# Reordering the opening, the set-up products and the last pair's pieces of a convolution block

## The chip, the cores and the metric

The kernel runs on one NeuronCore of a Trainium2 chip. The core has five engines that run their own instruction streams and meet through semaphores: TensorE (PE, matrix products from SBUF into PSUM), VectorE (DVE), ScalarE (ACT), GpSimd (POOL) and SyncE (SP). The last three, and in this kernel ScalarE at two places, also issue DMA transfers. The metric is the time of one execution on the device in microseconds, the median of several runs. Everything is computed in float32.

## The reference

The input x has 16 images of 192 channels with 64 × 64 pixels. Two layers follow each other.

```python
# layer 0
h = ln2d(x)                                    # over channels
pg = conv1x1(h, in_proj_w, in_proj_b)          # 192 -> 384
projected, gate = split(pg, 2, axis=1)
projected = dwconv3(projected, dw_k)           # depthwise 3x3
scanned = directional_scan(projected, ...)     # four recurrences, left, right, down, up, mixed
local = dwconv3(projected, le_k)
mixed = (scanned + local) * sigmoid(gate)
mixed = gelu(batch_norm(mixed))                # statistics over all images and pixels
x = x + conv1x1(mixed, out_proj_w, out_proj_b)
h2 = ln2d(x)
x = x + conv1x1(gelu(conv1x1(h2, fc1_w, fc1_b)), fc2_w, fc2_b)   # 192 -> 768 -> 192
# layer 1
t = relu(bn(mean over pixels(x) @ w1.T))       # 48 values an image
wt = (t @ w2.T + b2)                           # a 3x3 kernel for each image and channel
out = depthwise conv of x with wt, masked to 4 of the 9 taps, + bias
```

The batch norm needs all images, so the work falls into a part before it and one after it. The kernels of layer 1 need the mean of a whole image, so an image pair's output can be made only when its last pixel of layer 0 is there.

## The kernel before, in words

The function is conv_block_kernel. Images are taken in eight pairs, and 64 channels of the one image lie in partitions 0 to 63, of the other in 64 to 127 (HALF); the index t counts three groups of 64 channels. The order of instructions on all engines is the one in which the program writes them (manual_schedule), so where a call stands in the text is where it stands in its engine's queue.

**First stage**, 64 chunks of 512 pixels of a pair. load_a (L463) brings a chunk in by six transfers, three on the sync queue and three on the GpSimd queue, into one of four xa buffers. turn (L476) transposes it on PE (L481). variance (L485, L488 and L489 on DVE) and deviation (L491: a square root on ACT, L493, and a reciprocal on DVE, L494) give the scale of the layer norm. project (L497) makes the products with the weights wi (L509 on PE), and DVE (L514) and ACT (L515) scale them out of PSUM into stg or mid, in turns of four chunks. store and store_first (L524, L530) write these to DRAM and to the tile low.

Ahead of the loop, projection_weights (L270) scales the weights by the norm's weight (L275, DVE), forms their mean over channels by products (L278, PE), and its result, called centre at L555, subtracts it (L279, DVE).

The other set-up work is spread over the chunks by a table: beside(n, f) puts f behind chunk n's own instructions. The entries that the change touches are these.

- decays (L281): sigmoid and tanh on ACT, six small DVE instructions, and an exponential on ACT, beside chunk 0. gains (L292), beside chunk 1, needs its results.
- sums_across(k) (L357): three transposes on PE (L360) into a PSUM tile from bank(), and a copy out by DVE (L361). conv_bias(k) (L363) is one product (L365, PE) and copies out (L317, DVE). They stand beside chunks 11 and 12, 13 and 14, 15 and 16.
- positions(k) (L394): three transposes on PE (L397) into a tile from bank(), and a copy by ACT (L399). It stands beside chunks 11, 13, 15, 17, 24, 26, 30 and 34. All of bank() is one PSUM bank.
- runs(t) (L382): DVE only, beside chunks 20 to 22.
- finish_weights (L131): with k = 0, beside chunk 50, the scale s1 of the squeeze on ACT and DVE and the share of the norm's bias in the hidden layer's bias by 18 products of one column (L139, PE) with an addition on DVE (L141); with k = 1 to 3, beside chunks 51 to 53, the scaling of wf1 by the norm's weight on DVE (L143).

**Second stage**, 96 steps k of two channels each, from k = −2. depthwise(k+2) (L602) makes products on PE (L612) from low, pg_o or mid into ps_d, and ACT adds the bias (L625, L627). tables(k+1) writes decay tables by ACT (L635), scans(k+1) runs two recurrences on DVE (L647, L649), local and vertical multiply on PE (L656, on quarters of the array: 64 rows by 64 columns), sigmoid is on ACT (L677), gate on DVE (L690, L691). The first depthwise needs what store_first wrote last into low (L527).

**Third stage**, 64 chunks again: out projection (L855, L859), norm (L882 to L910), the hidden layer first (L920, with ACT's L923) and second (L817), final (L941). At the end of a pair, pooled, squeeze and excite give the kernels (taps, L970).

**Last pair.** Its output is made after the loop by dynamic_last (L986), for four row groups g of 16 rows and three channel groups t, into a tile ol from a ring of four buffers (tag gl). With dg None, ACT makes the first tap with the bias (L995) and DVE adds three taps (L65, 128 × 1024 each). With dg, PE makes the piece by products with the taps on a 128 × 128 diagonal, eight products into two PSUM banks (ps_d, L1002), and ACT evicts them with the bias (L1003). Before, t = 2 is on PE and t = 0 and 1 are on DVE. Each piece leaves by two transfers (L1006), on the sync queue for DVE's pieces and on GpSimd for PE's.

```python
    dynamic_last(n_pairs - 1, 0, 0, None)
    for g in range(NG):
        dynamic_last(n_pairs - 1, g, 1, None)
        if g + 1 < NG:
            dynamic_last(n_pairs - 1, g + 1, 0, None)
        dynamic_last(n_pairs - 1, g, 2, dg)
```

Of the kernel before, what the change touches and what calls it, by code (L numbers as in the profile page):

```python
# [27 lines left out]
C = 192  # L28
HW = 64
# [26 lines left out]
def conv_block_kernel(ctx: ExitStack, tc: tile.TileContext, x, prm, w_in, w_out, w_fc1, b_fc1, w_fc2, w1, bn1, w2, out):  # L56
# [73 lines left out]

    def finish_weights(k, pb):  # L131

        if k == 0:
            nc.scalar.activation(s1, b1[:, 3:4], AF.Sqrt, bias=eps5[0:RED])
            nc.vector.reciprocal(s1, s1)
            nc.vector.tensor_mul(s1, s1, b1[:, 0:1])
            for m in range(NFC):
                for t in range(3):
                    nc.tensor.matmul(pb[:, m:m + 1], wf1[0:64, t, 128 * m:128 * m + 128],  # L139
                                     pt3[0:64, t, LN2B:LN2B + 1], start=(t == 0), stop=(t == 2))  # L140
            nc.vector.tensor_add(bf1, bf1, pb[:, 0:NFC])  # L141
        else:
            nc.vector.tensor_scalar_mul(wf1[:, k - 1], wf1[:, k - 1], pt3[:, k - 1, LN2W:LN2W + 1])  # L143

# [99 lines left out]
    with ExitStack() as stage:  # L244
# [22 lines left out]
        def bank():  # L267
            return psa.tile([128, CH], F32, tag="pb", name="pb")

        def projection_weights():  # L270

            by_group = lambda v: v.rearrange("p (k g c) -> p g k c", k=2, c=GC)
            flat = lambda v: v.rearrange("p g k c -> p (g k c)")
            for t in range(3):
                nc.vector.tensor_scalar_mul(wi[:, t], by_group(w0[:, t]), pt3[:, t, LN1W:LN1W + 1])  # L275
            pc = bank()
            for t in range(3):
                nc.tensor.matmul(pc[:, 0:2 * C], mean_w, flat(wi[lo, t]), start=(t == 0), stop=(t == 2))  # L278
            return lambda: [nc.vector.tensor_sub(flat(wi[:, t]), flat(wi[:, t]), pc[:, 0:2 * C]) for t in range(3)]  # L279

# [135 lines left out]
        def beside(n, f, *args):  # L416
            side.setdefault(n, []).append((f, args))

        beside(0, decays)
        beside(1, gains)  # L420
# [8 lines left out]
        for k in range(3):  # L429
            beside(11 + 2 * k, sums_across, k)  # L430
            beside(12 + 2 * k, conv_bias, k)
        for k, n in enumerate((9, 11, 13, 15, 19, 24, 28, 32)):
# [13 lines left out]
        beside(49, load_lm, 1)  # L446
        beside(50, lambda: finish_weights(0, bank()))
        for k in range(3):
            beside(51 + k, finish_weights, k + 1, None)

# [98 lines left out]
        for c in range(3):  # L549
            load_a(c)  # L550
        centre = projection_weights()
        turn(0)
        for g in range(AR):
            variance(0, g)
        centre()  # L555
        deviation(0)
# [24 lines left out]
    with ExitStack() as stage:  # L581
# [163 lines left out]
        for k in range(-2, n_bp + 1):  # L745
# [14 lines left out]
            if 0 <= k + 1 < n_bp:  # L760
                scans(k + 1)
            if k + 2 < n_bp:
                depthwise(k + 2)
            if 0 <= k < n_bp:
                local(k)
                sigmoid(k)
            if k == n_bp - 5 * hp_:
                spread(0)
# [216 lines left out]

    def dynamic_last(p, g, t, dg):  # L986

        xi, taps, r = ximg[p % n_img], pst[p]["taps"], g * GR
        o = wp.tile([128, GR, HW], F32, tag="gl", name="ol", bufs=4)
        src = lambda k, r0, nr: xi[:, t, r0 + k // 3:r0 + k // 3 + nr, k % 3:k % 3 + HW]  # L990
        if dg is None:
            for k in range(NTAP):
                w = taps[:, t, k:k + 1]
                if k == 0:
                    nc.scalar.activation(o, src(k, r, GR), AF.Identity, bias=pt3[:, t, BIAS:BIAS + 1], scale=w)  # L995
                else:
                    stt(o, src(k, r, GR), w, o)
        else:
            ps = ps2.tile([128, 2, CH], F32, tag="f1", name="ps_d", bufs=2)
            for h in range(2):  # L1000
                for k in range(NTAP):
                    nc.tensor.matmul(rows(ps[:, h]), dg[:, k], src(k, r + h * CR, CR), start=(k == 0), stop=(k == NTAP - 1))  # L1002
            nc.scalar.activation(o.rearrange("p h w -> p (h w)"), ps.rearrange("p k n -> p (k n)"), AF.Identity,  # L1003
                                 bias=pt3[:, t, BIAS:BIAS + 1])
        for i, q in enumerate(HALF):
            (nc.sync if dg is None else nc.gpsimd).dma_start(ov[2 * p + i, 64 * t:64 * t + 64, r * HW:(r + GR) * HW],  # L1006
                                                             o[q].rearrange("p h w -> p (h w)"))

# [51 lines left out]

    dg = mxs[0].rearrange("p t n -> p (t n)")[:, 0:NTAP * 128].rearrange("p (k m) -> p k m", k=NTAP)
    for k in range(NTAP):
        nc.vector.tensor_scalar_mul(dg[:, k], ident, pst[n_pairs - 1]["taps"][:, 2, k:k + 1])
    dynamic_last(n_pairs - 1, 0, 0, None)
    for g in range(NG):
        dynamic_last(n_pairs - 1, g, 1, None)
        if g + 1 < NG:
            dynamic_last(n_pairs - 1, g + 1, 0, None)
        dynamic_last(n_pairs - 1, g, 2, dg)

# [41 lines left out]
```

## Time and profile before

The three runs before took 3830.37, 3835.88 and 3836.39 us; the median is 3835.88 us. The profiled execution has a span of 3826.1 us.

| stretch of the span | us from its start | PE busy | DVE busy | ACT busy | DMA share |
|---|---|---|---|---|---|
| opening | 0 to 20 | 7.38 of 20 | 5.48 | 1.55 | 0.96 |
| first stage | 200 to 400 | 198.69 of 200 | 155.10 | 80.77 | 0.98 |
| second stage | 800 to 1000 | 200.00 of 200 | 198.04 | 170.40 | 1.06 |
| third stage | 2000 to 3000 | 1000.00 of 1000 | 635.86 | 392.32 | 0.24 |
| end | 3790 to 3826 | 22.46 of 36 | 24.37 | 10.11 | 0.63 |

The DMA share is the mean busy share of the core's 16 DMA engines; values over 1 come from its reckoning. In the lines of the timeline and of the groups, an entry has the engine, the line of the program, the operation, the tile written and the tiles read with their shapes, and the number of instructions; what stands behind it in brackets is the idle time of the engine just before and what ended it. Each float32 product shows as two records on PE. The chain follows the work that ended last back from release to release.

### The profile page before, as it was taken

The numbers are of one execution on the slowest core, as the hardware profiler recorded it, in microseconds if no ns is written. First come the engines' busy times: TensorE is split into PE (matmuls) and PEld (weight loads), VectorE is DVE, ScalarE is ACT, GpSimd is POOL, SyncE is SP. The second block draws the span as 40 slices with busy tenths as digits, with TensorE's granted clock in tenths as the row PEclk, the third lists the DMA queues.
The fourth block names the chain that finished last, engine by engine and source line by source line (L and its number), as shares of the span: only waits on it lengthen the run. The fifth ranks groups of instructions, "written<-read, shape, count | busy, mean of one in ns | idle before, by whom it ended". The sixth has DMA issues, their size and how long they took to land.

```text
span 3826.1 us, 61482 instructions
## 1 busy us (share of the span) xinstructions
PE 3764.0 (98%) x25484; PEld 1762.9 (46%) x25484; DVE 2676.8 (70%) x4140; ACT 1780.3 (47%) x1879; POOL 420.2 (11%) x683
## 2 busy tenths in 40 slices
PE   8999999999999899999999999999999999999998
PEld 5566666776555433333333333333333333333333
DVE  6787776999999964556656656756665766674764
ACT  3343434888888733333434434434343433343342
POOL 2334332010010110000000000000000000000000
PEclk9999999999999999999999999999999999999999
DMA  6899998999999741112212212222222221221212
GB/s 158 227 252 238 275 263 254 296 283 274 285 275 268 209 91 34 43 39 73 74 48 61 77 53 64 64 67 60 64 56 67 70 63 49 79 72 39 69 28 72
DMA packets 307526, 491.14 MB, mean 128 GB/s; under 512 B 46432, under 2 KB 202416, under 8 KB 307248
## 3 DMA queue, kind: packets, MB, share of 16 engines
q1 hardware_dynamic: 249424, 294.88, 28.7%
q0 software_dynamic: 57408, 191.99, 18.9%
q8 instruction: 202, 3.31, 0.4%
q14 instruction: 76, 0.62, 0.1%
q10 hardware_dynamic: 416, 0.33, 0.0%
HBM read 284.91 MB, written 197.92 MB: 126 GB/s over the span
## 4 chain that ended last, share of the span: by engine, by line
PE 95%; DMA 2%; DVE 2%; issue 0%; ACT 0%; POOL 0%; SPq 0%; POOLq 0%; DVEq 0%; ACTq 0%
PE ps_f L920 27%; PE ps_f L817 26%; PE ps_pj L509 12%; PE ps_l L656 10%; PE ps_d L612 6%; PE ps_o L859 5%; PE ps_o L855 3%; PE ps_xt L481 2%; PE ps_v L882 1%; PE ps_m L882 1%; DMA xa<-in_x_dram 0%; PE ps_k L817 0%; DVE ol L65 0%; DVE v L647 0%; DMA ximg<-mixed_d 0%
## 5 line engine op out<-in xcount | busy, mean ns | idle before, releaser
L920 PE MATMUL ps_f<-h,wf 64*128 64x512 f32 x4608 | 1050.1, 600 | 5.1 <-DVE h L910 4.6
L817 PE MATMUL ps_f<-gl,place 128*64 128x512 f32 x4608 | 1021.5, 592 | 0.0
L923 ACT ACTIVATE gl<-ps_f,bf 128x1024 f32<-128x1024 f32 x384 | 428.0, 1115 | 1163.1 <-PE ps_f L920 1162.4
L920 PEld LDWEIGHTS ps_f<-h,wf 64*128 64x128 f32 x4608 | 433.5, 187 | 564.5 <-issue 563.2
L862 DVE SCALAR_TENSOR_TENSOR ximg<-ps_o,pt,low 128x256 f32<-128x256 f32 x384 | 168.3, 481 | 626.5 <-PE ps_o L859 623.7
L817 PEld LDWEIGHTS ps_f<-gl,place 128*64 128x64 f32 x4608 | 330.5, 137 | 580.0 <-issue 537.9
L509 PE MATMUL ps_pj<-wi,xa 64*128 64x384 f32 x3072 | 515.9, 488 | 3.4 <-DVE stg L514 3.4
L509 PEld LDWEIGHTS ps_pj<-wi,xa 64*128 64x128 f32 x3072 | 294.3, 187 | 197.1 <-issue 12.3
L65 DVE SCALAR_TENSOR_TENSOR o<-ximg,taps,o 128x1024 f32<-128x1024 f32 x252 | 323.8, 1285 | 85.7 <-ACT o L980 78.2
L984 POOL DMA_DIRECT2D out_dram<-o x168 | 87.9, 528 | 2134.1 <-DVE o L65 2131.3
L909 DVE RECIPROCAL rs<-rs 128x512 f32<-128x512 f32 x64 | 214.3, 3349 | 64.4 <-ACT rs L908 64.4
L647 DVE TENSOR_TENSOR_SCAN v<-tab,q 128x1024 f32<-128x1024 f32 x96 | 218.3, 2274 | 10.7 <-ACT tab L635 10.7
L649 DVE TENSOR_TENSOR_SCAN v<-tab,q 128x1024 f32<-128x1024 f32 x96 | 217.5, 2265 | 0.0
L635 ACT ACTIVATE tab<-mask,dec_b 128x1024 f32<-128x1024 f32 x192 | 209.0, 1138 | 0.0
L859 PE MATMUL ps_o<-low,wo 128*64 128x256 f32 x1536 | 209.0, 393 | 0.0
L515 ACT ACTIVATE stg<-ps_pj,rsa 128x384 f32<-128x384 f32 x128 | 120.2, 943 | 189.6 <-PE ps_pj L509 176.6
L515 ACT ACTIVATE mid<-ps_pj,rsa 128x384 f32<-128x384 f32 x128 | 120.9, 944 | 182.5 <-PE ps_pj L509 172.2
L488 DVE BATCH_NORM_STATS2 st<-ps_xt 128x6 f32<-128x192 f32 x512 | 173.9, 340 | 24.0 <-PE ps_xt L481 24.0
L891 DVE TENSOR_TENSOR h<-ximg,ps_m 128x768 f32<-128x768 f32 x128 | 116.1, 948 | 98.7 <-PE ps_m L882 98.7
L237 DVE STREAM_TRANSPOSE low<-low 128x512 f32<-128x512 f32 x174 | 167.6, 1014 | 2.1 <-issue 0.3
L469 POOL DMA_DIRECT2D xa<-in_x_dram x192 | 119.8, 630 | 369.1 <-PE ps_pj L509 308.3
L941 DVE SCALAR_TENSOR_TENSOR ximg<-ps_f,pt,ximg 128x512 f32<-128x512 f32 x192 | 134.1, 748 | 36.2 <-PE ps_f L817 35.8
(198 smaller groups left out, 4143.4 us busy)
## 6 DMA issues: line engine op xcount, KB each, us to landing
low<-in_x_dram SPq DMA_DIRECT2D x128, 384.0 KB
out_dram<-o POOLq DMA_DIRECT2D x168, 256.0 KB, 3.7
mid<-pg_d SPq DMA_DIRECT2D x8, 4096.0 KB
low<-mixed_d SPq DMA_DIRECT2D x116, 256.0 KB
low<-pg_d SPq DMA_DIRECT2D x7, 4096.0 KB
pg_o<-pg_d SPq DMA_DIRECT2D x7, 4096.0 KB
xa<-in_x_dram POOLq DMA_DIRECT2D x192, 128.0 KB, 6.1
xa<-in_x_dram SPq DMA_DIRECT2D x192, 128.0 KB
```

Of the source, the lines that this page charges most:

```text
L65: nc.vector.scalar_tensor_tensor(o, in0, scalar, in1, ALU.mult, ALU.add, **kw)
L509: nc.tensor.matmul(ps[i], pixels(n, t, g)[q], wi[q, t].rearrange("p g k c -> p (g k c)"), start=(t == 0), stop=(t == 2))
L515: nc.scalar.activation(stag[blk][1][:, :, j], ps[1], AF.Copy, scale=rs[:, g, 1:2])
L612: nc.tensor.matmul(dst(ps[o, ih]), mats[g % 2]["dm"][q, di + 1, :, ch], src(s["pg"][q, :, 0, ch]), start=(di == 0), stop=stop)
L647: nc.vector.tensor_tensor_scan(vf, tab, q, 0.0, ALU.mult, ALU.add)
L649: nc.vector.tensor_tensor_scan(vf[:, ::-1], tab[:, ::-1], q[:, ::-1], 0.0, ALU.mult, ALU.add)
L656: nc.tensor.matmul(dst(bst[k]["ps"][i][o]), lm_of(g)[q, m, :, c], src(q, ih), start=start, stop=stop)
L817: nc.tensor.matmul(ps[q], w(i), rhs(i), start=start, stop=stop)
L859: nc.tensor.matmul(ps[q, wh].rearrange("p (r w) -> p r w", w=32), wo[:, 64 * t:64 * t + 64], cols(rows(s["mx"][:, i]))[:, :, wh], start=Fa ...
L909: nc.vector.reciprocal(rs, rs)
L920: nc.tensor.matmul(pf[:, i], wf1[q, t, 128 * m:128 * m + 128], s["h"][q, t], start=(t == 0), stop=(t == 2))
L923: nc.scalar.activation(gl, pf, AF.Gelu, bias=bf1[:, m:m + 1])
```

## The change

The opening is put in another order: projection_weights becomes a generator that runs in three steps, and decays() runs ahead of the loop instead of beside chunk 0. sums_across and conv_bias move from chunks 11 to 16 to chunks 18 to 23, of which none has a positions. finish_weights is split in three: squeeze_scale stays beside chunk 50, hidden_bias (PE and DVE) goes to the beginning of the second stage, ahead of its first depthwise, and scale_hidden, now on ACT, goes to steps 1, 3 and 5 of the second stage. In the last pair PE makes seven pieces and DVE five. PE's pieces are made by products on quarters of the array: 16 of 64 rows by 64 columns with the diagonal's halves, where the two halves of the rows of pixels go to the two halves of the PSUM partitions. Such a piece leaves by four transfers, over two queues; the last three use ScalarE's and sync's queues, the others GpSimd's and sync's. The purpose is to fill or shorten the times in which PE waits.

```diff
-    def finish_weights(k, pb):
-        if k == 0:
...
-        else:
-            nc.vector.tensor_scalar_mul(wf1[:, k - 1], wf1[:, k - 1], pt3[:, k - 1, LN2W:LN2W + 1])
+    def squeeze_scale():
+        nc.scalar.activation(s1, b1[:, 3:4], AF.Sqrt, bias=eps5[0:RED])
+        nc.vector.reciprocal(s1, s1)
+        nc.vector.tensor_mul(s1, s1, b1[:, 0:1])
+    def hidden_bias(pb):
+        for m in range(NFC):
+            for t in range(3):
+                nc.tensor.matmul(pb[:, m:m + 1], wf1[0:64, t, 128 * m:128 * m + 128],
+                                 pt3[0:64, t, LN2B:LN2B + 1], start=(t == 0), stop=(t == 2))
+        nc.vector.tensor_add(bf1, bf1, pb[:, 0:NFC])
+    def scale_hidden(t):
+        nc.scalar.activation(wf1[:, t], wf1[:, t], AF.Copy, scale=pt3[:, t, LN2W:LN2W + 1])
@@ projection_weights
             for t in range(3):
                 nc.vector.tensor_scalar_mul(wi[:, t], by_group(w0[:, t]), pt3[:, t, LN1W:LN1W + 1])
+            yield
             pc = bank()
             for t in range(3):
                 nc.tensor.matmul(pc[:, 0:2 * C], mean_w, flat(wi[lo, t]), start=(t == 0), stop=(t == 2))
-            return lambda: [nc.vector.tensor_sub(flat(wi[:, t]), flat(wi[:, t]), pc[:, 0:2 * C]) for t in range(3)]
+            yield
+            for t in range(3):
+                nc.vector.tensor_sub(flat(wi[:, t]), flat(wi[:, t]), pc[:, 0:2 * C])
+            yield
@@ the table
-        beside(0, decays)
         beside(1, gains)
...
-            beside(11 + 2 * k, sums_across, k)
-            beside(12 + 2 * k, conv_bias, k)
+            beside(18 + 2 * k, sums_across, k)
+            beside(19 + 2 * k, conv_bias, k)
...
-        beside(50, lambda: finish_weights(0, bank()))
-        for k in range(3):
-            beside(51 + k, finish_weights, k + 1, None)
+        beside(50, squeeze_scale)
@@ ahead of the chunks
-        centre = projection_weights()
+        steps = projection_weights()
+        next(steps)
+        decays()
         turn(0)
+        next(steps)
         for g in range(AR):
             variance(0, g)
-        centre()
+        next(steps)
         deviation(0)
@@ second stage
             if 0 <= k + 1 < n_bp:
                 scans(k + 1)
+            if k == -2:
+                hidden_bias(psb.tile([128, CH], F32, tag="l", name="pb_h", bufs=4))
             if k + 2 < n_bp:
                 depthwise(k + 2)
             if 0 <= k < n_bp:
                 local(k)
                 sigmoid(k)
+            if k in (1, 3, 5):
+                scale_hidden(k // 2)
@@ dynamic_last
             ps = ps2.tile([128, 2, CH], F32, tag="f1", name="ps_d", bufs=2)
-            for h in range(2):
-                for k in range(NTAP):
-                    nc.tensor.matmul(rows(ps[:, h]), dg[:, k], src(k, r + h * CR, CR), start=(k == 0), stop=(k == NTAP - 1))
+            for k in range(NTAP):
+                for i, q in enumerate(HALF):
+                    for h in range(2):
+                        nc.tensor.matmul(rows(ps[HALF[h], i]), dg[q, k, q], src(k, r + h * CR, CR)[q],
+                                         start=(k == 0), stop=(k == NTAP - 1))
...
-        for i, q in enumerate(HALF):
-            (nc.sync if dg is None else nc.gpsimd).dma_start(...)
+        for i in range(2):
+            if dg is None:
+                nc.sync.dma_start(ov[2 * p + i, 64 * t:64 * t + 64, r * HW:(r + GR) * HW], o[HALF[i]].rearrange("p h w -> p (h w)"))
+            for h in range(2 if dg is not None else 0):
+                r0 = r + h * CR
+                queues[h].dma_start(ov[2 * p + i, 64 * t:64 * t + 64, r0 * HW:(r0 + CR) * HW],
+                                                  o[HALF[h], i * CR:(i + 1) * CR].rearrange("p h w -> p (h w)"))
@@ after the loop (last = n_pairs - 1)
+    dg2 = taps_on_diagonals(0)
+    dynamic_last(last, 0, 0, None)
+    dg1 = taps_on_diagonals(1)
+    dynamic_last(last, 1, 0, None)
+    dynamic_last(last, 0, 2, dg2)
+    dynamic_last(last, 1, 2, dg2)
+    dynamic_last(last, 2, 0, None)
+    dynamic_last(last, 2, 2, dg2)
+    dynamic_last(last, 3, 0, None)
+    dynamic_last(last, 3, 2, dg2)
+    dynamic_last(last, 0, 1, None)
+    for g in range(1, NG):
+        dynamic_last(last, g, 1, dg1, (nc.scalar, nc.sync))
```

More of the change, by code (lines that the diff above doesn't have):

```diff
@@ L129, in load_weights @@
                 nc.sync.dma_start(pv[q, 1], prm[128:C])
-    def finish_weights(k, pb):
-        if k == 0:
[L134 to L141, printed above, removed]
-        else:
-            nc.vector.tensor_scalar_mul(wf1[:, k - 1], wf1[:, k - 1], pt3[:, k - 1, LN2W:LN2W + 1])
+    def squeeze_scale():
[10 more added lines that the diff above has]
+        nc.scalar.activation(wf1[:, t], wf1[:, t], AF.Copy, scale=pt3[:, t, LN2W:LN2W + 1])
     n_blk = n_half * NB
@@ L984, in dynamic, with dynamic_last @@
             nc.gpsimd.dma_start(ov[2 * p + i, 64 * t:64 * t + 64, r * HW:(r + GR) * HW], o[q].rearrange("p h w -> p (h w)"))
-    def dynamic_last(p, g, t, dg):
+    def dynamic_last(p, g, t, dg, queues=(nc.gpsimd, nc.sync)):
         xi, taps, r = ximg[p % n_img], pst[p]["taps"], g * GR
@@ L999, in dynamic_last @@
             ps = ps2.tile([128, 2, CH], F32, tag="f1", name="ps_d", bufs=2)
-            for h in range(2):
-                for k in range(NTAP):
-                    nc.tensor.matmul(rows(ps[:, h]), dg[:, k], src(k, r + h * CR, CR), start=(k == 0), stop=(k == NTAP - 1))
+            for k in range(NTAP):
[3 more added lines that the diff above has]
+                                         start=(k == 0), stop=(k == NTAP - 1))
             nc.scalar.activation(o.rearrange("p h w -> p (h w)"), ps.rearrange("p k n -> p (k n)"), AF.Identity,
                                  bias=pt3[:, t, BIAS:BIAS + 1])
-        for i, q in enumerate(HALF):
-            (nc.sync if dg is None else nc.gpsimd).dma_start(ov[2 * p + i, 64 * t:64 * t + 64, r * HW:(r + GR) * HW],
-                                                             o[q].rearrange("p h w -> p (h w)"))
+        for i in range(2):
[5 more added lines that the diff above has]
+                                                  o[HALF[h], i * CR:(i + 1) * CR].rearrange("p h w -> p (h w)"))
     def at(f, n, *a):
@@ L1059, in conv_block_kernel, with taps_on_diagonals @@
         at(bn_gelu, late_)
[L1061 to L1069, printed above, removed]
+    last = n_pairs - 1
+    def taps_on_diagonals(j):
+        dg = mxs[j].rearrange("p t n -> p (t n)")[:, 0:NTAP * 128].rearrange("p (k m) -> p k m", k=NTAP)
+        for k in range(NTAP):
+            nc.vector.tensor_scalar_mul(dg[:, k], ident, pst[last]["taps"][:, 2 - j, k:k + 1])
+        return dg
+    dg2 = taps_on_diagonals(0)
[11 more added lines that the diff above has]
+        dynamic_last(last, g, 1, dg1, (nc.scalar, nc.sync))
 def _layout(i):
```

## The prediction

> **What bounds the kernel.** I read the page's busy time and chain first, then the busy time of stretches of 20 us, then the timeline and the chain at the four places that the change touches.
>
> ```profile
> PE 3764.0 (98%) x25484; PEld 1762.9 (46%) x25484; DVE 2676.8 (70%) x4140; ACT 1780.3 (47%) x1879; POOL 420.2 (11%) x683
> PE 95%; DMA 2%; DVE 2%; issue 0%; ACT 0%; POOL 0%; SPq 0%; POOLq 0%; DVEq 0%; ACTq 0%
> ```
>
> TensorE (PE) is busy 98% of the span and 95% of the chain. So time is won only where PE idles, or runs work that needn't be on its path: at the opening, beside some chunks of the first stage, at the seam to the second stage, and after the last chunk. The first is seen in the timeline (start, duration, engine, line, then the idle time before it and who ended it):
>
> ```profile
> 8.86 4.21 PE L278 MATMUL pb<-wi,wf 64*128 64x384 f32 x6 [8.86 <-DVE wi L275]
> 12.99 2.82 PE L481 MATMUL ps_xt<-ident,xa 128*128 128x128 f32 x12
> 19.58 2.80 PE L481 MATMUL ps_xt<-ident,xa 128*128 128x128 f32 x12 [3.76 <-DVE st L488]
> 22.30 9.25 PE L509 MATMUL ps_pj<-wi,xa 64*128 64x384 f32 x48
> ```
>
> PE starts at 8.86, runs the mean products before the first transposes, then sits 3.76 us while VectorE (DVE) takes chunk 0's variances. The next view is the chain in chunks 10 to 13 (start, duration, what):
>
> ```profile
> 131.96 7.99 PE ps_pj L509 x48
> ...
> 140.68 0.33 ACT rsa L493
> 141.01 0.03 issue
> 141.03 0.20 DVE rsa L494
> 141.24 0.22 DVE wf L361
> ...
> 141.50 0.40 PE pb L397 x3
> 141.90 1.46 PE ps_xt L481 x12
> 143.36 7.94 PE ps_pj L509 x48
> 151.30 0.52 PE pb L365 x2
> ```
>
> A plain chunk is 7.94 + 1.46 = 9.40 us. Here L397 waits for a PSUM bank whose reader, the copy L361, stands behind the reciprocal, so PE leaves its own work for ACT and DVE. The chain around chunk 50 shows the bias products of finish_weights:
>
> ```profile
> 511.06 7.94 PE ps_pj L509 x48
> 518.99 3.91 PE pb L139 x35
> 522.90 2.45 PE ps_xt L481 x12
> 525.35 8.58 PE ps_pj L509 x48
> ```
>
> and the timeline the seam and the end:
>
> ```profile
> 649.52 9.17 PE L612 MATMUL ps_d<-low,dm 64*64 64x512 f32 x110 [2.20 <-DMA low<-mid]
> 3783.19 29.27 PE L1002 MATMUL ps_d<-ximg,low 128*128 128x512 f32 x64 [0.75 <-PE ps_k L817]
> 3784.03 30.80 DVE L65 SCALAR_TENSOR_TENSOR ol<-ximg,taps,ol 128x1024 f32<-128x1024 f32 x24 [0.46 <-ACT ol L995]
> 3798.09 1.24 ACT L995 ACTIVATE ol<-ximg,pt,taps 128x1024 f32<-128x1024 f32 x1 [3.89 <-DMA out_dram<-ol]
> 3813.52 1.11 ACT L1003 ACTIVATE ol<-ps_d,pt 128x1024 f32<-128x1024 f32 x1 [4.35 <-DMA out_dram<-ol]
> ```
>
> PE and DVE end there together (3812.5 and 3814.8), but ACT waits for output buffers too.
>
> **What the Trainium skill says.** "TensorEngine Tiling (Array Packing)", section Tiling Modes: in 64×64 mode there are four tiles that run in parallel. The trace agrees: L656 is of this kind, and its chain pieces are 36 records in 3.86 us, 0.107 us each, against 0.43 us between L1002's weight-load pairs, 0.215 each, at full width. "TensorE: Matmul & The Clock Gate", section Part 1: after an idle window of about 3.4 us the array runs at half rate until about as long a busy one. It agrees: chunk 0's and 1's transposes take 2.8 us against 1.46, and L1002's first pairs are 0.85 us apart. "DMA: Bandwidth & Descriptors", section on the anatomy of one DMA: about 2.0 us of a transfer's time is fixed, whatever its size. The trace has 4.4 to 5.1 us from a GpSimd issue of 256 KB to landing, which is consistent with it.
>
> **The change, part by part.**
>
> Opening. Order on PE becomes transposes of chunk 0, mean products, transposes of chunk 1. The sync queue's own issues show when chunk 0's three pieces land, as each of the issues at 9.40, 11.37 and 13.51 waited for one. So the first transposes go piece by piece and end at 13.5 + 0.9 = 14.4 instead of 15.8. Mean products: 14.4 to 18.6 at the half rate of before (4.2). The variances (3.7 us, 8 x 0.46) run beside them, 14.4 to 18.1. The centring needs the products, so its first third ends at 19.1, hidden by chunk 1's transposes: 18.6 to 21.4 cold, 20.1 warm. Chunk 0's projection then starts at 20.1 to 21.4 against 22.30, and a PE without the 3.76 us gap should be warm sooner, worth up to the 1.24 us by which L509's first chunk (9.18) exceeds 7.94. Bounds 0.9 and 3.4; I take 2.2. decays() moves ahead of the transposes: its six DVE instructions (1 us) and two table loads (1.28 us each) run before 13.5, while DVE and ACT have nothing to do; chunk 2's 0.57 us excess (9.97 against 9.40), which a table load in front of L493 caused, goes. Together −2.8, bounds −1.5 and −4.
>
> Sums across. With sums_across and positions in one chunk the period is 11.40 (131.96 to 143.36), 11.39 and 11.40: 2.00 over plain. A chunk with positions alone (195.91 to 205.49) is 9.58, 0.18 over. So chunks 11, 13, 15 win 3 x 1.82 = 5.5. The moved sums cost 0.2 to 0.3 each in chunks 18, 20, 22, where no second user waits for the bank: +0.8. The conv_bias products cost 0.52 a chunk before and after. DVE has room for runs() there: it is 70 to 80% busy in this stage. Net −4.7.
>
> Hidden bias. Chunk 50 took 14.29 us and chunk 51 10.04 instead of 9.40: −5.5 in all, because the one-column products leave the clock low. At the seam they wait for the same release as depthwise(0) did, the last eviction of the first stage at 646.13, and take 4.1 us: depthwise then starts at 650.3, instead of 649.52 with 0.8 us of it already done. Cost +1.6, as 2.5 of the 4.1 us lie in the wait for low<-mid. Net −3.9. What is queued behind them on PE is depthwise alone; the addition to bf1 on DVE has nobody waiting.
>
> Scaling of wf1. Three DVE multiplications leave chunks 51 to 53, where DVE has slack: 0. Three ACT instructions enter the second stage at k = 1, 3, 5. Nearest row: L923, 1024 elements in 1.115 us, so about 0.9 each. Behind each stand tables(k+2) on ACT, and scans(k+2) on DVE wait for them; ACT is 74% busy in 600 to 800 us, PE carries the chain. +0.3, bounds 0 and 2.7.
>
> End. PE's pieces go from 4 to 7, each 16 quarter products, 32 records of 0.107 = 3.4 us instead of 7.3, and 7 of them are 24 us with about 1.7 more cold. DVE's go from 8 to 5 of 3.85 us: 19.3 plus two sets of diagonals of 0.87. So both engines could be done by 3808. But a piece holds one of four buffers until its output has landed. From the timeline the DVE pieces land about 6.3 us after their last operation (3791.8 to 3798.09, 3799.4 to 3805.79), PE's 5 to 6 after theirs. Buffer time before: 8 x (1.2 + 3.9 + 6.3) + 4 x (1.1 + 6) = 119.6; after: 5 x 11.4 + 7 x (1.1 + 6.6) = 110.9, where 1 us is for the sync queue, on which half of each PE piece waits behind a DVE piece. Over four buffers: 29.9 against 27.7, −2.2; bounds 0 (1.3 us more on the landing of each of the seven PE pieces would undo it) and −6 (both engines free). I take −2.
>
> First stage's transfers. DMA share is 0.9 to 1.07 from 200 to 520 us, and PE there lost twice 1.7 us to late stores. What chunks 11 to 16 save comes off a stretch (140 to 200) with 12% DMA slack, 7 us; the moved work gives 2 us of room back at 205 to 255. Chunk 50's stall let the queues catch up (share 0.63 at 520 to 540), which ends. +1, bounds 0 and 5.
>
> Sum: −2.8 − 4.7 − 3.9 + 0.3 − 2 + 1 = −12.1. 3835.9 − 12.1 = 3823.8.
>
> **Rivals.**
> Handed back to DMA: the saving beside the chunks reappears as waits for stores near 340, 490 and 530 us, and the end doesn't move. For it: share near 1. Against: PE idled only 3.4 us there. The opening, 2.8, and about 2 of the rest stay: 3831.
> More than summed: the array warm at 14 us (−4 instead of −2.8), the end bound by engines (−6), transfers not in the way: −4 − 4.7 − 3.9 − 6 + 0 = −18.6, 3817. For it: the end's DMA share is only 0.69. Against: the buffer waits of 3.9 to 4.4 us.
> Slower: everything in the first stage is handed back, the bias costs its 1.6 at the seam, each of the three scalings stalls the scans (+2.7), and 14 more issues in the end, in order on sync, push the last landing by 4: +8.3, 3844. For it: the sync queue serves both kinds of pieces. Against: PE idles in the seam in plain sight, and DVE has slack at the start of the second stage.
>
> **Numbers.** Main case 0.71 at 3824; handed back 0.14; more 0.10; slower 0.05. 0.2% is 7.7 us, a bound at 3828.2. Faster: 0.69 of main, 0.04 of handed back, 0.10 = 0.83; within: 0.02 + 0.10 + 0.02 = 0.14; slower 0.03. The range takes in most of the handed-back case and nearly the more case, whose middles are 3831 and 3817: 3816 to 3831.
>
> **What would show it.** Right: L509 starts its first chunk at 20 to 21.5; no period over 10 us at chunks 11 to 16; chunk 50 plain; depthwise starting near 650.3 less what is won before; from the taps (L970 at 3782.49) to the start of the last eviction (3813.52) 28 to 30 us instead of 31.0, with ACT still waiting on out_dram<-ol. Wrong: longer store waits before L514 or L515, DVE waiting for tab at k = 3, 5, 7, or quarter products over 0.15 us a record. The end is the least certain step.

## The result, and the profile after

The changed kernel takes 3814.14 us (median of 4 runs, 3810.24 to 3820.33) against 3836.14 us (4 runs, 3830.37 to 3838.59) of the kernel before: a ratio of 0.9946, 95% interval 0.9928 to 0.9965. In microseconds that is −21, interval −28 to −13. It is faster, as forecast, and by more: 3824.0 was forecast, with a range from 3816 to 3831, and the median lies just below that range.

The two profiled executions differ by less than the medians, 3826.1 and 3814.8 us of span, −11.3. The profiled execution of the kernel before took 3827.9 us, less than any of its timed ones; the section on chunks 25 to 50 shows where. The page's busy time and the chain's shares of the changed kernel:

```profile
PE 3764.5 (99%) x25644; PEld 1719.9 (45%) x25644; DVE 2665.5 (70%) x4132; ACT 1779.2 (47%) x1881; POOL 420.1 (11%) x683
PE 96%; DMA 1%; DVE 1%; ACT 0%; issue 0%; POOL 0%; SPq 0%; ACTq 0%; POOLq 0%
```

PE has as much busy time as before (3764.5 against 3764.0): the 11 us came out of its waits, and what single places saved in PE work others added. The page can't say more, since every part of the change is a tenth of a per cent. So I cut the timelines of PE, ACT and DVE at points that both kernels have, and took the stretches between them, for the two kernels and for a second profiled execution of the changed one (called again below). A chunk starts with its transposes here, and a seam is the passage from one stage to the next:

| stretch, us | before | after | again | forecast difference |
|---|---|---|---|---|
| start to chunk 5's transposes | 60.3 | 58.7 | 59.0 | −2.8 |
| chunk 5 to 11 | 60.4 | 60.4 | 60.4 | 0 |
| chunk 11 to 25 | 139.7 | 134.7 | 134.7 | −4.7 |
| chunk 25 to 50 | 239.8 | 242.8 | 247.8 | +1 |
| chunk 50 to 54 | 43.1 | 37.6 | 37.6 | −5.5 |
| chunk 54 to the end of the last projection | 101.8 | 101.8 | 101.8 | 0 |
| last projection to the last scan (seam, second stage) | 679.1 | 683.2 | 681.5 | +1.9 |
| last scan to the first square of the third stage | 26.7 | 26.8 | 26.7 | 0 |
| first square to the last pair's taps | 2431.5 | 2432.2 | 2430.6 | 0 |
| taps to the last transfer | 39.0 | 35.1 | 34.7 | −2 |
| last transfer to the end of the span | 4.7 | 1.5 | 1.5 | not in the forecast |

Five stretches shrink and two grow. The views behind them follow, in the order of the prediction. Lines move by a few between the kernels: L484 of after is L481 of before, L512 is L509, L281 is L278, L618 is L612.

The timeline of PE in the opening (start, duration, engine, line, then the idle time before it and who ended it):

```profile
13.64 1.09 PE L484 MATMUL ps_xt<-ident,xa 128*128 128x128 f32 x4 [1.05 <-DMA xa<-in_x_dram]
14.66 4.20 PE L281 MATMUL pb<-wi,wf 64*128 64x384 f32 x6
18.79 2.82 PE L484 MATMUL ps_xt<-ident,xa 128*128 128x128 f32 x12
21.54 9.06 PE L512 MATMUL ps_pj<-wi,xa 64*128 64x384 f32 x48
```

The wait of 3.76 us is gone, yet the first projection starts at 21.54 instead of 22.30: chunk 1's transposes take 2.82 us again and the projection 9.06. The array is as cold as it was: later chunks' transposes take 1.46 us. And the mean products, which ran while chunk 0 was still being loaded, from 8.86 on, now stand behind that loading, from 14.66 on: much of the gap was moved and not removed.

The chain in chunks 13 to 15:

```profile
130.43 7.94 PE ps_pj L512 x48
138.37 0.17 PE pb L403 x3
138.54 1.46 PE ps_xt L484 x12
140.00 7.94 PE ps_pj L512 x48
147.94 1.46 PE ps_xt L484 x12
```

ACT and DVE have left the chain there: a chunk with positions (L403) is 9.57 us, not 11.40. And the chain around chunk 50:

```profile
507.54 7.94 PE ps_pj L512 x48
515.48 1.46 PE ps_xt L484 x12
516.94 7.94 PE ps_pj L512 x48
```

It is plain, 9.40 us a chunk. The 36 products now stand at the seam (timeline):

```profile
637.06 6.89 PE L140 MATMUL pb_h<-pt,wf 64*128 64x1 f32 x36 [1.04 <-ACT mid L518]
643.88 10.26 PE L618 MATMUL ps_d<-low,dm 64*64 64x512 f32 x120
```

They take 6.89 us where 4.1 was forecast, and the depthwise products behind them 10.26 (120 records), where before had 9.17 for its last 110, after a wait. The end (timeline of PE and ACT):

```profile
3778.86 15.45 PE L1014 MATMUL ps_d<-ximg,low 64*64 64x512 f32 x128 [0.75 <-PE ps_k L827]
3793.65 1.11 ACT L1016 ACTIVATE ol<-ps_d,pt 128x1024 f32<-128x1024 f32 x1 [3.87 <-DMA out_dram<-ol]
3794.82 10.53 PE L1014 MATMUL ps_d<-ximg,low 64*64 64x512 f32 x96 [0.51 <-ACT ol L1016]
3805.69 1.11 ACT L1016 ACTIVATE ol<-ps_d,pt 128x1024 f32<-128x1024 f32 x1 [4.40 <-DMA out_dram<-ol]
3808.67 1.11 ACT L1016 ACTIVATE ol<-ps_d,pt 128x1024 f32<-128x1024 f32 x1 [1.86 <-DMA out_dram<-ol]
```

From the taps (3778.15) to the start of the last eviction it is 30.5 us, against 31.0 before: hardly less. Most of what became shorter lies behind it.

### The profile page after: what moved, and what is told of

Same layout as the page of the kernel before. It is cut to its first block, busy times and chain, and to the rows that moved or that the text cites. A ratio compares the mean times of both kernels' runs of the same rounds, so it can differ in the third digit from the quotient of the medians.

```text
span 3814.8 us, 61825 instructions
## 1 busy us (share of the span) xinstructions
PE 3764.5 (99%) x25644; PEld 1719.9 (45%) x25644; DVE 2665.5 (70%) x4132; ACT 1779.2 (47%) x1881; POOL 420.1 (11%) x683
## 4 chain that ended last, share of the span: by engine, by line
PE 96%; DMA 1%; DVE 1%; ACT 0%; issue 0%; POOL 0%; SPq 0%; ACTq 0%; POOLq 0%
PE ps_f L930 27%; PE ps_f L827 26%; PE ps_pj L512 13%; PE ps_l L662 11%; PE ps_d L618 6%; PE ps_o L869 5%; PE ps_o L865 3%; PE ps_xt L484 2%; PE ps_v L892 1%; PE ps_m L892 1%; DMA xa<-in_x_dram 1%; PE ps_k L827 0%; DMA ximg<-mixed_d 0%; DMA mixed_d<-mid 0%; DVE v L653 0%
## 5 line engine op out<-in xcount | busy, mean ns | idle before, releaser
L512 PE MATMUL ps_pj<-wi,xa 64*128 64x384 f32 x3072 | 516.0, 489 | 4.9 <-DVE stg L517 4.8
L512 PEld LDWEIGHTS ps_pj<-wi,xa 64*128 64x128 f32 x3072 | 293.6, 188 | 199.3 <-issue 12.8
```

What stands on the lines that cost most here:

```text
L512: nc.tensor.matmul(ps[i], pixels(n, t, g)[q], wi[q, t].rearrange("p g k c -> p (g k c)"), start=(t == 0), stop=(t == 2))
```

## The experiments

My theory after the result: the chunks win what was forecast, the seam costs more because the one-column products run cold, the end wins more than forecast, and chunks 25 to 50 are scatter of transfers that has nothing to do with the change. The rivals: transfers hand back part of the saving; or the end's gain is not the end's at all.

### The changed kernel once more, and the end alone

again is the changed kernel unchanged. end_alone is the kernel before with the end of the changed one.

```diff
-    def dynamic_last(p, g, t, dg):
+    def dynamic_last(p, g, t, dg, queues=(nc.gpsimd, nc.sync)):
 ...
+    dg2 = taps_on_diagonals(0)
+    dynamic_last(last, 0, 0, None)
+    dg1 = taps_on_diagonals(1)
 ...
+        dynamic_last(last, g, 1, dg1, (nc.scalar, nc.sync))
```

> The changed kernel once more, unchanged, for more executions and a second profile. Theory 'as in the profiled pair': its parts are -9 us by the end of the first stage, +4.6 at the seam to the second, 0 in the middle and -7 in the end, -11.4 in all, and the medians' -22 is partly the draw of executions: the new difference of medians lies at -10 to -18. Theory 'more than the pair shows': the change wins 20 us or more in every execution, and the new profile shows at least 15 of it at one or two places. The prediction's sum was -12.1.

> The kernel before with only the new end: seven pieces of the last pair on quarters of the array, five on VectorE, four transfers a piece, the last three over ScalarE's and sync's queues. Theory 'pair': -7 us, of which 3.8 before the last landing (38.7 to 34.9 us from the taps) and 3.2 after it (4.9 to 1.8). The prediction's buffer sum: -2, with nothing after the landing. If the end is worth 10 or more, the missing part of the medians' difference is here.

Measured: again 3817.07 us (5 runs, 3815.07 to 3818.34), ratio 0.9954 (0.9942 to 0.9966), so −18 against 3834.0 of before on that chip, interval −22 to −13 (the medians differ by −17, within the first theory's −10 to −18; no place of the new profile has the 15 us of the second). end_alone 3828.08 us (19 runs), ratio 0.9982 (0.9976 to 0.9989): −7, interval −9 to −4. From its taps to the last transfer are 34.7 us (before 39.0), from there to the end 1.55 (before 4.7), together −7.4. So the end alone is worth some 7 us, more than three times the −2 of the forecast, and the timed runs and the stretches agree on it.

end_alone has the first stage of before, and its chunks 25 to 50 took 249.4 us where before took 239.8. The same code differs by 9.6 us there from one execution to another.

### The last three pieces back on the GpSimd queue

```diff
-        dynamic_last(last, g, 1, dg1, (nc.scalar, nc.sync))
+        dynamic_last(last, g, 1, dg1)
```

> The changed kernel, but its last three pieces leave over GpSimd's and sync's queues like the others. Theory 'the stretch after the last landing belongs to the GpSimd queue': it goes back from 1.8 to about 4.9 us, and the time rises by 3 to 4. Rival 'it belongs to nothing of the queues': it stays under 2.5 us, and the time rises by 0 to 1, as GpSimd's issue is about 0.3 later.

Measured: 3819.38 us, ratio 0.9963 (0.995 to 0.9976), which the timing can't tell from again. The stretches can. First the changed kernel's last microseconds (window and its length, ACT's busy time and instructions, the granted clock, the DMA share, GB/s), then those of end_gpsimd and of before, whose spans are 3814.8, 3815.7 and 3826.1:

```profile
3812.00:3813.00 1.00, 0.00 (x0) 0.50 0.86 291
3813.00:3814.00 1.00, 0.00 (x0) 0.50 0.02 6
```

```profile
3810.00:3811.00 1.00, 0.00 (x0) 0.50 0.45 146
3811.00:3812.00 1.00, 0.00 (x0) 0.50 0.00 0
3812.00:3815.00 3.00, 0.00 (x0) 0.50 0.00 0
```

```profile
3821.00:3822.00 1.00, 0.00 (x0) 0.50 0.06 21
3822.00:3824.00 2.00, 0.00 (x0) 0.50 0.00 0
3824.00:3826.00 2.00, 0.00 (x0) 0.50 0.00 0
```

After the last transfer the program needs 1.5 us to end in the changed kernel, 4.9 with its last pieces on GpSimd's queue, 4.7 before. Taps to last transfer is 34.8 in end_gpsimd, against 34.7 in again. So some 3 us of the gain hang on which queue the last pieces take.

The traces also show what the program waits for there. At its end GpSimd runs a DRAIN, the longest of three (count, then the shortest, median and longest in ns, then the first and last start, for before, end_gpsimd and the changed kernel):

```profile
L1108 POOLq DRAIN  x3: 46/93/10015, 3815.3 to 3825.9; - x3
L1137 POOLq DRAIN  x3: 46/93/8201, 3806.8 to 3815.5; - x3
L1137 POOLq DRAIN  x3: 46/93/7707, 3798.5 to 3814.5; - x3
```

The long one is the first. It starts at GpSimd's last DMA issue and takes 7.5 to 10.0 us in the thirteen executions, 7.7 in ten of them. In before and end_gpsimd it ends at 3825.4 and 3815.0, 0.8 us ahead of the program's end, while SyncE had seen all landings at 3822.3 and 3811.4. In the changed kernel it is over at 3806.2, and the landings, seen by 3814.0, set the end. So the gain hangs on how late GpSimd issues its last transfer, not on a slower landing of its queue.

### The old split of the last pair

quarters_old_split keeps quarter products and the queue of the last piece, but puts the pieces in the old order, 4 on PE and 8 on DVE.

```diff
-    dg1 = taps_on_diagonals(1)
-    dynamic_last(last, 1, 0, None)
 ...
+    for g in range(NG):
+        dynamic_last(last, g, 1, None)
+        if g + 1 < NG:
+            dynamic_last(last, g + 1, 0, None)
+        dynamic_last(last, g, 2, dg2, (nc.scalar, nc.sync) if g == NG - 1 else (nc.gpsimd, nc.sync))
```

> Changed kernel with the last pair's pieces in the old order and the old split, 4 on TensorE and 8 on VectorE; TensorE's are quarter products still, and the last goes out on ScalarE's and SyncE's queues. Theory A (the end is won by taking three pieces from VectorE): VectorE is bound again by 8 x 3.85 = 30.8 us, taps to the last transfer 37.5 to 39 as before against 34.7, the closing stretch 1.6, total 3 to 4 us above the changed kernel. Theory B (shorter TensorE pieces, or the queues, win it): taps to the last transfer 34 to 36, total within 1.5 us of the changed kernel.

Measured: 3817.98 us, ratio 0.9962 (0.9948 to 0.9975); the total doesn't separate it from again. Taps to last transfer is 37.2 us, just under the 37.5 to 39 of theory A and clearly over the 34 to 36 of theory B, and over the 34.7 to 35.1 that the eight executions with the changed end and queues have; the closing stretch is 1.2. DVE is busy with its 24 taps without a break again, 30.79 us, as before. So of the 4.1 us between 39.0 and about 34.9, 1.7 come with the quarter products and their transfers on two queues, and 2.4 with the split 7 to 5 and its order of pieces; before and quarters_old_split have one profiled execution each.

### The bias products back in chunk 50

```diff
+        beside(50, lambda: hidden_bias(bank()))
 ...
-            if k == -2:
-                hidden_bias(psb.tile([128, CH], F32, tag="l", name="pb_h", bufs=4))
```

> The changed kernel with the bias products of the hidden layer back beside chunk 50. Theory 'the seam gave back most of it': chunk 50 becomes 14.3 us and chunk 51 10.0 again (+5.5), the stretch from the last product of the first stage to the first local product goes from 17.9 to 13.3 us (-4.6), together +1. The prediction's step (seam cost 1.6): +3.9.

Measured: 3819.67 us, ratio 0.9961 (0.9948 to 0.9973), 2.6 above again, with intervals that overlap. By stretches, chunks 50 to 54 take 43.1 us against 37.6, and last projection to last scan 680.3 against 681.5 to 683.2. The chain around its chunk 50:

```profile
518.99 4.11 PE pb L140 x35
523.10 2.75 PE ps_xt L485 x12
```

Moving the products is worth −5.5 there, and costs +1.2 to +2.9 at the seam by this comparison. The products take 0.12 us each here, where at the seam of the changed kernel they take 0.19. In the kernel before, with the same place for them, the granted clock is 1.00 from 519 to 523 us, under the products, and 0.53 from 523 to 526, behind them.

Why two costs at the seam? PE's busy time and granted clock in two windows of 7 us from the last projection on, first after, then again, then before:

```profile
637.00:644.00 7.00, 6.94 (x40) 0.58 0.71 196
644.00:651.00 7.00, 7.00 (x72) 0.69 1.10 374
```

```profile
641.00:648.00 7.00, 5.96 (x37) 0.74 0.51 133
648.00:655.00 7.00, 7.00 (x86) 0.78 1.06 359
```

```profile
645.00:652.00 7.00, 3.69 (x24) 0.82 0.58 152
652.00:659.00 7.00, 7.00 (x108) 0.94 1.09 370
```

The trace's record of the clock has only 0.5 and 1 there, so a mean c over 7 us is 14 × (1 − c) us at half rate: 5.9 + 4.3 = 10.2 us after, 3.6 + 3.1 = 6.7 again, 2.5 + 0.8 = 3.4 before. These are three, two and one times 3.4 us; in the record itself the spells are 10.24, 6.83 and 3.41 us long. "TensorE: Matmul & The Clock Gate" of the Trainium skill, section on what is actually happening (Part 1), says that activity is watched in windows of 3.4 us that run freely and don't start with the kernel; the three numbers agree with it. So against before the products cost one or two cold windows more, 1.7 us each. In all thirteen executions the first seam has two (two executions) or three (five) cold windows with the products, and none (bias_tail), one (four) or two (tail_buffers) without. That the phase of the windows decides within each group is argued from this, no run controlled it. In the changed kernel's first seam (last projection to first local product) that gives 16.3 and 16.4 us in two executions (again, sums_old) and 18.0 in five; before has 13.4. Up to the last scan it is +2.4 or +4.0 us.

### The opening and the sums, put back one at a time

```diff
+        beside(0, decays)
 ...
-        decays()
-        turn(0)
         next(steps)
+        turn(0)
```

> Changed kernel with the opening alone put back: decays() beside chunk 0 and the mean products ahead of the first transposes. Theory (the opening's win is 1.0 us up to the first projection and 0.6 us more by chunk 5, because the array stays cold in either order): the first projection chunk starts at 22.3 instead of 21.54 and lasts 9.2, chunk 2's transposes start at 31.5 instead of 30.5, chunk 5's at 60.3 instead of 58.7. Rival (the order has no part in it, the 1.6 us are scatter of loads): chunk 5 stays at 58.5 to 59. The total can't show it: 1.6 us lie inside the store waits' scatter.

```diff
-            beside(18 + 2 * k, sums_across, k)
-            beside(19 + 2 * k, conv_bias, k)
+            beside(11 + 2 * k, sums_across, k)
+            beside(12 + 2 * k, conv_bias, k)
```

> Changed kernel with sums_across and conv_bias back beside chunks 11 to 16, where positions() stand too. Theory (one PSUM bank shared by two users in one chunk is the whole of it): chunks 11, 13 and 15 take 11.4 us again, 18 to 23 are plain at 9.4 to 9.6, so that chunk 18's transposes start 7 us later than in the changed kernel and chunk 25's 5 us later, 258.5 to 259.5 instead of 253.8. Rival (the set-up work costs its own PE time wherever it stands): chunk 25 within 1.5 us of 253.8.

opening_old (one execution, 3826.93 us): the first projection starts at 21.36 and takes 9.66, chunk 2 starts at 30.9, chunk 5 at 59.7. It isn't the 22.3 and 60.3 that I expected, and the executions with the new opening differ as much among themselves: chunk 5 starts at 56.1 to 59.8 in ten of them, mean 58.2; with the old one at 60.3, 59.0 and 59.7. So the order is worth about 1.4 us on the mean, within a scatter of 3.7. Where it comes from: the first projection starts at 20.0 to 22.6 with the new order (mean 21.7) and at 21.4 to 22.3 with the old (mean 21.9), hardly a difference; but chunk 3 (chunk 2 in the prediction, which counts by projections) takes 9.97 us, from its transposes to the next, in all three executions with decays() beside chunk 0, and 9.40 in the ten others. The timeline of opening_old shows that the wait is back, with the mean products ahead of the transposes, and that chunk 1's transposes start at 18.64 all the same, in the changed kernel at 18.79:

```profile
12.30 2.57 PE L485 MATMUL ps_xt<-ident,xa 128*128 128x128 f32 x12
18.64 2.79 PE L485 MATMUL ps_xt<-ident,xa 128*128 128x128 f32 x12 [3.77 <-DVE st L492]
21.36 9.66 PE L513 MATMUL ps_pj<-wi,xa 64*128 64x384 f32 x48
```

sums_old (one execution, 3815.14 us): its chain in chunk 13 is that of before again.

```profile
136.55 0.27 ACT rsa L496
...
137.05 0.22 DVE wf L367
...
137.32 0.40 PE pb L403 x3
137.71 1.46 PE ps_xt L484 x12
```

Chunks 11 to 25 take 139.6 us against 134.7 in both executions of the changed kernel: 4.9, where 5 was expected. Its chunk 25 nevertheless starts at 256.2, not at 258.5 to 259.5, because this execution had the fastest opening of all (chunk 5 at 56.1).

### Other places for the bias products

bias_seam2 puts them, in two halves, around batch_norm(1) at the end of the second stage, and the scalings at the first iteration of the third. bias_tail puts the halves behind the local products of the second stage's last two steps.

```diff
-            if k == -2:
-                hidden_bias(psb.tile([128, CH], F32, tag="l", name="pb_h", bufs=4))
-            if k in (1, 3, 5):
-                scale_hidden(k // 2)
 ...
+        hidden_bias(pb_h, (0, 1, 2))
         spread(1)
         turn_back(y_low, mxs[0], 0, 1)
         batch_norm(1)
+        hidden_bias(pb_h, (3, 4, 5))
```

In bias_tail the second part of the edit is this instead:

```diff
+            if k == n_bp - 2:
+                pb_h = psb.tile([128, 2, CH], F32, tag="d", name="pb_h", bufs=2)[:, 0]
+                hidden_bias(pb_h, (0, 1, 2))
+            if k == n_bp - 1:
+                hidden_bias(pb_h, (3, 4, 5))
```

> Changed kernel with the one-column bias products moved from the first seam to the end of the second stage, in two halves of 18 products around batch_norm(1), and the three scalings of wf1 on ScalarE at the first iteration of the third stage. Theory (the bias products cost 3 to 4.6 us at the first seam because they run cold and leave the depthwise cold; at the second seam they stand in a wait of PE's that is there anyway): first seam, from the last projection to the first local product, 13.3 instead of 16.3 to 18; second seam longer by 0 to 1.5; in all 1.5 to 4.5 us below the changed kernel. Rival (the array is cold at the second seam as well and somebody waits for batch_norm or bf1 there): second seam longer by 3 or more, total within 1 us of the changed kernel.

> Changed kernel with the one-column bias products behind the local products of the last two steps of the second stage, where TensorE has no depthwise products left to make, 18 in each, into a depthwise bank; the scalings of wf1 on ScalarE at the first iteration of the third stage. Theory (a place where TensorE is warm and idle exists, so the products can cost nothing): first seam as before the change, last projection to first local product 13 to 13.4; second seam, last scan to the first square, 26.7 to 27.2 instead of the 29.97 that the halves around batch_norm(1) took; last projection to taps 3137.5 to 3139 if the second input group lands within 25 us of the last projection, up to 3140.5 if it lands at 26 to 28 as in the two kernels that had no bias products at the first seam; changed kernel: 3138.8 to 3142.1. Rival (the products on TensorE delay what VectorE takes up next at the tail): second seam 29 or more, last projection to taps 3142 or more.

bias_seam2: 3817.18 us, ratio 0.996 (0.9948 to 0.9973), no better than again; the rival's numbers were right, though no wait for batch_norm or bf1 is shown. The first seam is 13.1 us as hoped, but last projection to last scan is 681.7, and the second seam is 30.0 instead of 26.7. Two lines of its timeline say where both went:

```profile
669.83 2.53 PE L619 MATMUL ps_d<-pg_o,dm 64*64 64x512 f32 x17 [2.95 <-ACT tab L642]
1334.45 3.99 PE L140 MATMUL pb_h<-pt,wf 64*128 64x1 f32 x18
```

PE idles 2.95 us in front of the first product that reads pg_o. The trace names ACT, but ACT had copied the bank free by 666.5; what came at that moment is the part of the load of pg_o that GpSimd issued at 654.1, with 15.5 us to landing, 669.6. In the kernel before the same part was issued at 655.8 and landed 13.7 later, 669.5, and PE read it at 669.69: it came just in time. So in this execution the shorter seam only brought PE to the next wait. And the second half of the products ran cold in front of the output projections.

bias_tail: 3825.23 us on a chip on which before took 3843.81, ratio 0.9952 (0.9937 to 0.9966). Both of its halves run warm, between local products:

```profile
1323.92 2.17 PE L140 MATMUL pb_h<-pt,wf 64*128 64x1 f32 x18
1330.75 2.17 PE L140 MATMUL pb_h<-pt,wf 64*128 64x1 f32 x18
```

The second seam is 26.8 us, last projection to taps 3138.9 us, where the changed kernel has 3138.8 or 3142.1; the first pg_o product starts 26.3 us after the last projection, against 27.5 or 29.1. tail_buffers below, with the products at the same place, has 3138.8 and 28.3. So here the products delay nothing that the trace shows, yet the place wins 3.2 us or nothing, by which execution of the changed kernel it is compared with, and PE idles 2.8 us in front of its first pg_o product there too. In the total it doesn't show: chunks 25 to 50 took 257.2 us in this execution.

### More output buffers in the end

end_buffers is the changed kernel with five further buffers, cut from a tile that is free by then; tail_buffers has this and bias_tail together.

```diff
+    spare_o = [low[:, i * 2 * CH:(i + 1) * 2 * CH].rearrange("p (h w) -> p h w", w=HW) for i in range(3)]
+    spare_o += [low[:, (6 + 3 * i) * CH:(8 + 3 * i) * CH].rearrange("p (h w) -> p h w", w=HW) for i in range(2)]
 ...
-        o = wp.tile([128, GR, HW], F32, tag="gl", name="ol", bufs=4)
+        o = spare_o[len(made) - 5] if 5 <= len(made) < 10 else wp.tile([128, GR, HW], F32, tag="gl", name="ol", bufs=4)
```

> Changed kernel in which five of the last pair's twelve pieces (the fifth to the ninth) write into further output buffers, cut from a tile that is free by then, and the others keep the ring of four. Theory A (the end is bound by pieces that hold one of four buffers until their output has landed): the waits of ScalarE on out_dram<-ol in the last 30 us go, taps to the last transfer falls from 34.7 to between 29 and 32, total 3 to 5 us below the changed kernel. Theory B (the rate at which 6.3 MB leave, or VectorE's 5 x 3.85 us with its diagonals, binds): the waits go but the last transfer still ends 33.5 to 35 after the taps, total within 1.5 us of the changed kernel.

> Both of the other two kernels of this call in one: bias products at the tail of the second stage, five further output buffers in the end. If both theories hold the effects add: 4 to 8 us below the changed kernel, 3809 to 3813; if the end is bound by its transfers and not by its buffers, 0 to 3 below it, 3814 to 3817.

Taps to last transfer is 32.5 us in end_buffers and 32.2 in tail_buffers, 2.5 less than with four buffers: theory B's 33.5 is undershot, theory A's 32 just missed. Up to 1.2 us before the last eviction it is PE that sets the pace then (timeline of end_buffers):

```profile
3791.07 26.23 PE L1019 MATMUL ps_d<-ximg,low 64*64 64x512 f32 x224 [0.74 <-PE ps_k L827]
```

All seven pieces run without a break, and the last eviction follows 1.2 us after them, behind ScalarE's own DMA issues, which end at 3818.26. By time, end_buffers is 3816.99 us and tail_buffers 3821.26, with before at 3843.81 on that chip: ratios 0.9939 (0.9924 to 0.9955) and 0.9949 (0.9933 to 0.9964). Neither can be told from the changed kernel's 0.9946 and 0.9954. If there is a version better than it, it is by the 2.5 us of the end, which the stretches show and the totals don't.

### Chunks 25 to 50

No experiment was made for them, but all thirteen executions have the stretch. With the first stage of before: 239.8 (before), 249.4 (end_alone). With the changed one, or all but one part of it: 241.6, 242.2, 242.8, 244.4, 247.2, 247.8, 248.8 and 251.4, and 249.4, 255.5 and 257.2 on the chip on which before took 3843.8. PE waits there two or three times for transfers, near chunks 33, 46 and 50. Means are 244.6 and, without the last three, 245.8. So a hand-back of the saving to the transfers isn't seen; one of up to some 5 us could hide in this scatter, as the first mean is of two executions only.

## Why the prediction was right or wrong

**Opening**, −2.8 (bounds −1.5 and −4): the order did what was said, and the projection's start at 21.54 lies just past the 20.1 to 21.4. The step that failed is that a PE without the gap should be warm sooner: in the profiled execution chunk 1's transposes took 2.82 us and the first projection 9.06, cold both. Over thirteen executions it is about −1.4, of which −0.57, the excess that goes with decays() beside chunk 0, is the part that every execution shows. The term was mis-sized by half.

**Sums across**, −4.7: right. −5.0 over chunks 11 to 25 in both executions, undone by sums_old.

**Hidden bias**: chunk 50's share right, −5.5 forecast, −5.5 measured. The seam was mis-sized: +1.6 forecast for it, +2.4 or +4.0 measured up to the last scan. The step that failed is "take 4.1 us ... depthwise then starts at 650.3": the products took 6.04 to 6.89 us, because the clock fell under them, and the depthwise products behind started cold. I had priced them from chunk 50, where an array at full clock went into them, and had left out at the seam what the same paragraph says of chunk 51, that they leave the clock low.

**Scaling of wf1**, +0.3: no wait of DVE or PE for it is seen; the second stage's difference is accounted for by the cold windows.

**First stage's transfers**, +1: not confirmed and not refuted, 244.5 against 245.8.

**End**, −2 (bounds 0 and −6): this is the step that failed. It measured −3.9 up to the last transfer, −3.1 behind it, −7 in all, past the larger bound, and end_alone's timed runs say −7 as well. The prediction followed the buffers to the last eviction and put what lies behind it, the last transfers and the program's close, at nothing. The part that it followed, 31.0 to 30.5 us, moved least. Before, DVE ended 32.3 us after the taps (3814.83), its last transfers 6.6 us later; now DVE is done at 3804.6, and the last piece is one of PE's, whose transfers are over 4.6 us after its eviction begins (before 7.9). So −0.5 − 3.4 − 3.1. In before two paths ended together, and the sum had only one of them. DVE, with 30.80 us without a break, wasn't held by buffers; quarters_old_split, which brings 30.79 us of DVE back, loses 2.4. PE's last piece was held by a buffer, 4.35 us up to its eviction at 3813.52; its transfers landed with DVE's last, and GpSimd's DRAIN behind them, which the program waited for, ended 3.1 us after SyncE was ready. The sum itself also charged too much: 6.3 and 6.6 us of landing were assumed, and those that can be read off ACT's waits in the changed kernel are 5.4, 4.6, 5.4 and 4.9; only PE's first piece, half of which stood behind DVE's on the sync queue, took 10.3. The last eviction, finally, waits for no buffer, although the trace names a DMA: it stands behind ScalarE's own DMA issues, 3806.83 to 3808.49, the second of which began as that DMA landed, 3807.99; its buffer had been free since 3806.86.

With the measured terms the sum is −1.4 − 5.0 − 5.5 + 2.4 to 4.0 − 7.0 = −14.9 to −16.5, which is 3819 to 3821 and inside the forecast's range. The changed kernel's own measurement is 3814.1, with an interval of some 7 us to each side, and again's ratio on 3835.9 gives 3818.3 with 4.5 to each side. So between 3824.0 and 3814.1 the failed step accounts for −5, and the others together for +0.6 to +2.2, in the other direction, so that the errors in part cancel; the rest, 5 to 7 us, is within what these runs scatter by, and I can't attribute it.

Of the rivals, "more than summed" was nearest by its number (3817), and its term for the end (−6) nearest too, but for another reason: not that engines became the bound, but that the tail behind the last eviction became shorter. That its number is near is luck: its opening (−4) didn't happen. "Slower" fell. Of "handed back to DMA" one half fell, as the end moved; the other isn't seen, as chunks 25 to 50 scatter by more than what it hands back, and could hide there.

## What to carry to other kernels

An end is over when its last transfer has landed and the program has closed, so follow each engine's last piece past the last instruction that waits for a buffer, to its landing and to the last instruction of the engine that issues it. Where GpSimd needs 7.5 to 10 us from its last issue to its end, as here, give the last pieces to other queues. A few one-column products cost more than their number of records says, because the clock falls under them and stays low for what follows; the cheapest place found here was between other products of a warm array, in the last steps of the second stage, though no total showed the gain. When one profiled execution of the same code differs by 10 us in a stretch from the next, compare parts by stretches that don't contain it.

## What the runs showed of the hardware that I had not expected

- The time from the last transfer to the end of the program was 4.7 and 4.9 us in the two kernels whose last transfers include some of GpSimd's queue, and 1.2 to 1.7 us in the others. GpSimd's DRAIN, 7.5 to 10.0 us from its last issue on, accounts for it: in all thirteen executions the program ends 0.8 us after the later of this DRAIN and SyncE's last wait for a landing.
- PE was busy 6.94 of 7 us by the profile and yet its granted clock was 0.58: the 36 records of one column didn't hold the clock up. The spells at half rate were 3.4, 6.8 and 10.2 us long.
- Two halves of 18 such products took 2.17 us each while local products ran around them, and 3.99 us behind an idle stretch.
- Chunks 25 to 50 of the first stage, the same code in each, took from 239.8 to 257.2 us in thirteen executions. This spread of 17.4 us is as large as the whole effect of the change.
